# A state space layer on one core: sums moved to identity matmuls and ScalarE copies, ScalarE's work set between exponentials

## The chip, the cores and the metric

The kernel runs on one core of a Trainium2 chip. Its engines work side by side: PE (TensorE, matmuls into PSUM), DVE (VectorE), ACT (ScalarE), POOL (GpSimd), and SP, which here issues the transfers. They pass data through SBUF and PSUM and wait for each other by semaphores. The metric is the device time of one execution in microseconds (us), the median of several.

## The reference

Two layers work one after the other on four images of 384 channels and 64 x 64 positions, in float32. Only the first, a state space layer, is touched by the change. Cut to what matters:

```python
x = x + L0(group_norm(x))
x = x + L1(group_norm(x))            # attention over 7x7 neighbourhoods

def L0(x):                           # L = 4096 positions, D_INNER = 768, D_STATE = 16
    xn = layer_norm(x)
    xb, z = split(xn @ in_proj_w.T)
    xc = silu(causal_conv(xb, 4 taps) + conv_b)
    dt, Bm, Cm = split(xc @ x_proj_w.T)            # 24, 16, 16
    dt = softplus(dt @ dt_w.T + dt_b)
    A = -exp(A_log)
    def step(h, dt_t, B_t, C_t, x_t):              # along the positions
        h = exp(dt_t * A) * h + (dt_t * x_t) * B_t
        return h, sum_n(h * C_t)
    y = scan(step) + xc * D
    return (y * silu(z)) @ out_proj_w.T
```

## The kernel before

The first layer goes through each image in 16 chunks ("steps") of T = 256 positions, 64 steps in all. Channels lie on the partitions, 128 at a time, so the inner width is d = 0..5. For each d the 16 states are taken four at a time (g = 0..3): that makes 24 units m in a step, each of two halves of two states, and 48 "slots". Each slot holds two exponentials and two scans; all other work of the layer, for this chunk and for those before and after it, is put into the slots by a table, and each engine runs it in this order.

The core of a unit:

```python
def driven(I, m, h, eng):       # db = (dt * x) * B, on VectorE or GpSimd
    db = w2.tile([P, NG, T], F32, tag="db", bufs=6)
    dtx = dtx_ps[:, d % 2, :] if eng is nc.vector else h["dtx"][d]
    eng.tensor_tensor(db, dtx.broadcast(...), h["B"][g], ALU.mult)          # L550

def decay(I, m, half, h):       # two exponentials, into one of two PSUM tiles
    da = ps_a.tile([P, 2, T], F32, tag="da")                                # bufs=2
    for k in range(2):
        act(da[:, k, :], h["dt"][d // 2][:, d % 2, :], AF.Exp, scale=nega[:, d, n : n + 1])

def scans(I, m, half, hs):
    for k in range(2):
        nc.vector.tensor_tensor_scan(hs[:, j, :], da[:, k, :], dbs[I, m][:, j, :],
                                     state[:, d, n : n + 1], ALU.mult, ALU.add)  # L571

def with_c(I, m, h, hs):        # on GpSimd
    nc.gpsimd.tensor_copy(state[:, d, g * NG : (g + 1) * NG], hs[:, :, T - 1])   # L580
    nc.gpsimd.tensor_tensor(hs, hs, h["C"][g], ALU.mult)                         # L581

def summed(I, m, h, hs):        # sum over the states: accumulating transposes, L594
    ...

for n in range(STEPS * M):                       # M = 24 units
    I, m = divmod(n, M)
    hs = w2.tile([P, NG, T], F32, tag="hs", bufs=5)
    for half in range(2):
        decay(*nxt, steps[nxt[0]])               # of the half after this one
        if half == 0:
            with_c(*behind[-1])                  # of the unit before this one
            ...                                  # summed() of the unit before that
        scans(I, m, half, hs)
        run(I, 2 * m + half, 2 * m + half + 1)   # what the table has in this slot
```

Softplus, once for each pair of d (q = 0, 1, 2), as max(v, 0) + ln(1 + exp(-|v|)), with what rounding lost in 1 + exp put back:

```python
def project():   # PE: pb = w_dt x dt                                        L491
def parts():     # ACT: e = Abs(pb + bias), r = Relu(pb + bias), for k = 0, 1
def exped():
    act(t["e"], t["e"], AF.Exp, scale=-1.0)
    act(t["pb"], t["e"], AF.Identity, bias=1.0)
def logged():
    act(t["dt"], t["pb"], AF.Ln)
def lost():
    nc.vector.scalar_tensor_tensor(t["pb"], t["pb"], -1.0, t["e"],
                                   ALU.add, ALU.subtract)                 # L514
    nc.vector.tensor_tensor(t["pb"], t["r"], t["pb"], ALU.subtract)       # L517
def added():
    nc.vector.tensor_tensor(t["dt"], t["dt"], t["pb"], ALU.add)           # L520

at(first, project); at(first + 3, parts); at(first + 4, exped)
at(first + 5, logged); at(first + 6, lost); at(first + 7, added)          # first = 34, 36, 46
```

The dt of a pair then goes to GpSimd, too (dtx = dt * xc, L537), and a copy of dtx to PSUM for VectorE (L543). The output projection ends with the residual:

```python
def residual(first, n):
    xo = h["xo"][:, first : first + n, :]
    nc.vector.tensor_tensor(xo, h["po", first][:, :n, :], xo, ALU.add)    # L653
```

Once in a step ScalarE does all its Silu together (`burst`, slot 26): a table load, six instructions of 128x512, and a load of the table with Exp and Ln again. PSUM tiles for everything but da, y and dtx come from one pool of four banks.

Of the kernel before, what the change touches and what calls it, by code (L numbers as in the profile page):

```python
# [14 lines left out]
P = 128  # L15
C = 384
# [32 lines left out]
def two_layers(  # L49
# [74 lines left out]
    make_identity(nc, ident)  # L124
    ones_c = const.tile([P, P], F32, name="ones_c")
# [145 lines left out]
    def layer0(x1s, mvs, gms1):  # L271

        with ExitStack() as es:
# [8 lines left out]
            gms, gbs, st1s = {}, {}, {}  # L282
            dtx_ps = ps_x.tile([P, 2, T], F32, name="dtx_ps")

# [45 lines left out]
            def normed(I, h, at):  # L330
# [10 lines left out]
                def by_group():  # L341
                    h["xn"] = w2.tile([P, NJ, T], F32, tag="xn", name=f"xn_{b}_{i}", bufs=1)
                    for j in range(NJ):
                        act(
                            h["xn"][:, j, :], h["x"][:, j, :], AF.Identity,
                            scale=gms[b][:, j, 1:2], bias=gbs[b][:, j, :],
                        )
# [17 lines left out]

                def root():
                    act(h["var"][:, 0, :], h["var"][:, 0, :], AF.Ln, bias=eps)
                    act(h["var"][:, 0, :], h["var"][:, 0, :], AF.Exp, scale=-0.5)

                at(12, load)  # L370
                at(22, by_group)
                at(24, lambda: mean("xn", "mu"))
                at(26, lambda: with_row("mu", ALU.subtract))
                at(30, square)
                at(31, lambda: mean("sq", "var"))
                at(34, root)
                at(35, lambda: with_row("var", ALU.mult))
# [16 lines left out]
            def with_bias(dst, pb, bias):  # L394

                for k in range(2):
                    act(dst[:, k, :], pb[:, k, :], AF.Identity, bias=bias[:, k : k + 1])

            def prepared(I, h, at):
# [22 lines left out]
                at(-11, kept)  # L422
                for p, (x, c, z) in enumerate((
                    ((-10, -9, -6), (1, 2, 5), (9, 10, 13)),
                    ((-6, -5, -2), (3, 4, 7), (12, 13, 16)),
                    ((-4, -3, 0), (7, 8, 11), (15, 16, 19)),
                )):
                    d = 2 * p
                    pair(("x", p), x, lambda pb, k, d=d: in_proj(pb, k, d + k, h["xn"]))
                    at(x[2], lambda p=p, d=d: with_bias(  # L430
                        xb[:, d : d + 2, KC - 1 :], h["pb"][("x", p)], binp[:, d : d + 2]
                    ))

                    def conv_out(p=p, d=d):
                        c = w2.tile([P, 2, T], F32, tag="xc", name=f"xc_{b}_{i}_{d}", bufs=6)
                        with_bias(c, h["pb"][("c", p)], cvb[:, d : d + 2])
                        h["xc"].append(c)

                    pair(("c", p), c, lambda pb, k, d=d: conv(pb, k, d + k))
                    at(c[2], conv_out)  # L440

                    def z_out(p=p, d=d):
                        z = w2.tile([P, 2, T], F32, tag="sz", name=f"sz_{b}_{i}_{d}", bufs=6)
                        with_bias(z, h["pb"][("z", p)], binp[:, ND + d : ND + d + 2])
                        h["sz"].append(z)

                    pair(("z", p), z, lambda pb, k, d=d: in_proj(pb, k, ND + d + k, h["xn"]))
                    at(z[2], z_out)
# [15 lines left out]
                def rows():  # L464
# [6 lines left out]
                    for tag in "BBBCBCCC":  # L471
# [7 lines left out]
                at(26, burst)  # L479
                at(28, lambda: x_proj((0, 1, 2)))  # L480
                at(29, lambda: x_proj((3, 4, 5)))
                at(32, rows)

                def softplus(q, first):
# [12 lines left out]
                    def parts():  # L497
                        t["e"] = w2.tile([P, 2, T], F32, tag="sp_e", name=f"spe_{b}_{i}_{q}")
                        t["r"] = w2.tile([P, 2, T], F32, tag="sp_r", name=f"spr_{b}_{i}_{q}")
                        for k in range(2):  # L500
                            bias = dtb[:, 2 * q + k : 2 * q + k + 1]
                            act(t["e"][:, k, :], t["pb"][:, k, :], AF.Abs, bias=bias)
                            act(t["r"][:, k, :], t["pb"][:, k, :], AF.Relu, bias=bias)

                    def exped():
                        act(t["e"], t["e"], AF.Exp, scale=-1.0)
                        act(t["pb"], t["e"], AF.Identity, bias=1.0)
# [5 lines left out]
                    def lost():  # L513
                        nc.vector.scalar_tensor_tensor(  # L514
                            t["pb"], t["pb"], -1.0, t["e"], ALU.add, ALU.subtract
                        )
                        nc.vector.tensor_tensor(t["pb"], t["r"], t["pb"], ALU.subtract)  # L517

                    def added():
                        nc.vector.tensor_tensor(t["dt"], t["dt"], t["pb"], ALU.add)  # L520
                        h["dt"].append(t["dt"])

                    at(first, project)
                    at(first + 3, parts)
# [640 lines left out]
```

## Time and profile of the kernel before

| | |
|---|---|
| time, median of 3 | 8366.12 us (8359.93 to 8367.44) |
| span of the profiled execution | 8357.8 us |
| busy: PE, DVE, ACT, POOL | 87%, 87%, 70%, 85% |
| transfers | 583.06 MB, mean 70 GB/s |
| L571, the scans | 5760 with a state to start from, 728 ns mean |
| L581, the product with C | 1536, 2358 ns mean |
| exponentials into da | 6144, 477 ns mean |

Busy time is the time in which at least one instruction of an engine runs. A group's line gives its line in the kernel, the engine and operation, what it writes and reads, the shapes and the count; after the bar the busy time in us and the mean length of one in ns; after the second bar the engine's idle time just before such instructions, and who ended it. The row PEclk is the granted clock of TensorE, as a share of full speed.

### The profile page before, as it was taken

To read this page: it belongs to the slowest core of one execution; us is meant where nothing else is said; L and a number is where in the kernel's file an instruction comes from. 1 tells how busy PE (TensorE), PEld (TensorE's weight loads), DVE (VectorE), ACT (ScalarE), POOL (GpSimd) and SP (SyncE) were. 2 spreads that over 40 slices of the span, in tenths; PEclk is the share of its full clock that TensorE was granted. 3 is DMA by queue.
4 is the path that set the end of the run, shared out by engine and by line. 5 is a ranking of instruction groups with operands and counts; after the bars stand their busy time and mean duration, and the time that the engine had idled before them with its cause. 6 is when DMAs were issued, how large, how long until landed. Compare 5 with 4: busy or idle time off the path is not lost. (4 is left out here: it accounts for less than half of the span.)

```text
span 8357.8 us, 139186 instructions
## 1 busy us (share of the span) xinstructions
PE 7252.0 (87%) x45882; PEld 5495.0 (66%) x45882; DVE 7311.7 (87%) x13300; ACT 5812.2 (70%) x13758; POOL 7092.7 (85%) x5719
## 2 busy tenths in 40 slices
PE   7888888888888888888888888888699999999999
PEld 5776677777666677776777677766555555555555
DVE  5999999999999999999999999999856666666666
ACT  5777777777777777777777777777545455455455
POOL 4999999999999999999999999999767677777677
PEclk9998898889889998899898889989799999999999
DMA  3111211121112111211211111112122232232222
GB/s 112 59 61 66 75 58 55 63 74 58 62 66 74 53 58 66 72 58 64 68 63 53 58 65 60 55 57 71 65 89 86 76 94 88 78 92 85 83 87 65
DMA packets 327504, 583.06 MB, mean 70 GB/s; under 512 B 62940, under 2 KB 211180, under 8 KB 326660
## 3 DMA queue, kind: packets, MB, share of 16 engines
q1 hardware_dynamic: 326788, 574.17, 21.3%
q8 instruction: 370, 6.06, 0.3%
q14 instruction: 346, 2.83, 0.1%
HBM read 471.49 MB, written 84.73 MB: 67 GB/s over the span
## 5 line engine op out<-in xcount | busy, mean ns | idle before, releaser
L571 DVE TENSOR_TENSOR_SCAN hs<-da,state,db 128x256 f32<-128x256 f32 x5760 | 3855.0, 728 | 88.9 <-ACT da L96 64.8
L96 ACT ACTIVATE da<-dt,nega 128x256 f32<-128x256 f32 x6144 | 2917.7, 477 | 1208.2 <-DVE hs L571 1100.8
L581 POOL TENSOR_TENSOR hs<-hs,C 128x1024 f32<-128x1024 f32 x1536 | 3621.7, 2358 | 123.9 <-POOL state L580 0.4
L594 PE MATMUL y<-ident,hs 128*128 128x128 f32 x12288 | 1774.6, 296 | 904.5 <-POOL hs L581 902.3
L594 PEld LDWEIGHTS y<-ident,hs 128*128 128x128 f32 x12288 | 1540.5, 153 | 1207.9 <-POOL hs L581 1098.9
L941 POOL TENSOR_SCALAR sg<-sg,rsum 128x308 f32<-128x308 f32 x1536 | 1619.9, 1073 | 633.8 <-DVE rsum L939 631.8
L550 POOL TENSOR_TENSOR db<-dtx,B 128x1024 f32<-128x1024 f32 x576 | 1360.5, 2362 | 0.1
L550 DVE TENSOR_TENSOR db<-dtx_ps,B 128x1024 f32<-128x1024 f32 x960 | 1141.3, 1199 | 0.0
L382 PE MATMUL mm_ps<-xn,w_in 128*128 128x256 f32 x4608 | 1127.4, 392 | 10.1 <-DVE yg L624 8.1
L96 ACT ACTIVATE sg<-sg,mx 128x308 f32<-128x308 f32 x1536 | 828.7, 541 | 251.3 <-DVE mx L926 236.7
L926 DVE CUSTOM_DVE_ANT_0 sg<-lg_ps,bias 128x308 f32<-128x308 f32 x1536 | 643.1, 475 | 375.1 <-PE lg_ps L920 375.1
L382 PEld LDWEIGHTS mm_ps<-xn,w_in 128*128 128x128 f32 x4608 | 872.5, 197 | 119.1 <-DVE yg L624 8.4
L389 PE MATMUL mm_ps<-xb,dcv 128*128 128x256 f32 x3072 | 783.9, 409 | 0.0
L389 PEld LDWEIGHTS mm_ps<-xb,dcv 128*128 128x128 f32 x3072 | 615.7, 208 | 88.3 <-issue 0.3
L969 ACT COPY tb<-pt_ps 88x512 f32<-88x512 f32 x384 | 222.2, 579 | 624.7 <-PE pt_ps L965 624.7
L580 POOL COPY state<-hs 128x4 f32<-128x4 f32 x1536 | 289.1, 188 | 341.8 <-DVE hs L571 328.0
L639 PE MATMUL mm_ps<-yg,w_out 128*128 128x256 f32 x2304 | 539.8, 385 | 0.0
L956 DVE COPY ta<-pt_ps 110x512 f32<-110x512 f32 x768 | 492.4, 682 | 23.2 <-PE pt_ps L951 23.2
L639 PEld LDWEIGHTS mm_ps<-yg,w_out 128*128 128x128 f32 x2304 | 439.6, 195 | 59.1
L951 PE MATMUL pt_ps<-ident,sg 128*110 128x128 f32 x3072 | 417.7, 279 | 0.8 <-POOL sg L941 0.8
L951 PEld LDWEIGHTS pt_ps<-ident,sg 128*110 128x110 f32 x3072 | 322.7, 133 | 77.9 <-issue 47.6
L824 PE MATMUL mm_ps<-xn,w_qkv 128*128 128x512 f32 (+2 forms) x612 | 270.7, 579 | 60.4 <-DVE xn L811 53.2
(141 smaller groups left out, 9152.5 us busy)
## 6 DMA issues: line engine op xcount, KB each, us to landing
B<-bcrows SPq DMA_DIRECT2D x256, 512.0 KB
C<-bcrows SPq DMA_DIRECT2D x256, 512.0 KB
vw<-vd SPq DMA_DIRECT2D x1792, 33.0 KB
xr<-x SPq DMA_DIRECT2D x28, 1056.0 KB
vd<-v SPq DMA_DIRECT2D x280, 96.0 KB
xi<-in_x_dram SPq DMA_DIRECT2D x64, 384.0 KB
xo<-in_x_dram SPq DMA_DIRECT2D x64, 384.0 KB
x<-xo SPq DMA_DIRECT2D x64, 384.0 KB
```

Of the source, the lines that this page charges most:

```text
L96: ins = nc.scalar.activation(o, i, func, **kw)
L382: nc.tensor.matmul(pb[:, k, :], w_in[:, j, m * P : (m + 1) * P], xn[:, j, :], start=(j == 0), stop=(j == NJ - 1),)
L389: nc.tensor.matmul(pb[:, k, :], dcv[:, d, c, :], xb[:, d, c : c + T], start=(c == 0), stop=(c == KC - 1),)
L550: eng.tensor_tensor(db, dtx.unsqueeze(1).broadcast_to([P, NG, T]), h["B"][g], ALU.mult)
L571: nc.vector.tensor_tensor_scan(hs[:, j, :], da[:, k, :], dbs[I, m][:, j, :], state[:, d, n : n + 1] if I % NCHUNK else 0.0, ALU.mult, ALU.add,
L581: nc.gpsimd.tensor_tensor(hs, hs, h["C"][g], ALU.mult)
L594: nc.tensor.matmul(y[:, d % 2, half, :], hs[:, k, half * P : (half + 1) * P], ident, is_transpose=True, start=(first and half == 0 and d % ...
L639: nc.tensor.matmul(h["po", first][:, m - first, :], w_out[:, d, m * P : (m + 1) * P], h["yg"][d // 2][:, d % 2, :], start=(d == 0), stop=( ...
L926: nc.vector.tensor_tensor_reduce(sg[:, hh, :], lg[:, :NK], bias[:, 4 * m + hh, :], -1.0, BIG, ALU.add, ALU.min, mx[:, hh : hh + 1],)
L941: nc.gpsimd.tensor_scalar(sg[:, hh, :], sg[:, hh, :], rs[:, hh : hh + 1], None, ALU.mult)
L951: nc.tensor.transpose(pt[: KN[c], col : col + P], sg[:, 2 * pair + hh, KOFF[c] : KOFF[c] + KN[c]], ident,)
L956: nc.vector.tensor_copy(t[: KN[0], :, :].rearrange("p a q -> p (a q)"), pt[: KN[0], :])
```

## The change

It takes additions off VectorE. In softplus the parts r, ln and minus the lost part are added up by matmuls with the identity (and with its negative, `nident`) in PSUM, and ScalarE copies the sum to SBUF. The residual, too, is a matmul with the identity, ahead of the output projection in the same accumulation, and ScalarE copies the result. ScalarE takes the copies of the last states from GpSimd. And the table of slots is new: ScalarE's work is cut into single instructions, each with its own slot, and set between the two exponentials of a slot.

```diff
+    nident = const.tile([P, P], F32, name="nident")
+    nc.vector.tensor_scalar(nident, ident, -1.0, None, ALU.mult)
...
+            AT = {
+             'norm': (9, 20, 21, 22, 22, 25, 28, 30, 32, 33, 33),
+             'kept': -11,
+             'x': ((-9, -8, -4, -4), (-6, -6, -3, -2), (-4, -4, -1, 1)),
+             'c': ((1, 1, 5, 6), (3, 4, 8, 8), (8, 9, 13, 13)),
+             'z': ((8, 9, 13, 13), (10, 11, 15, 15), (14, 15, 19, 21)),
+             'burst': (25, 26, 28, 31),
+             'softplus': ((32, 34, 36, 36, 37, 38, 40, 42), (34, 38, 39, 40, 42, 43, 44, 48),
+                          (45, 49, 50, 50, 51, 51, 52, 55)),
+             'dtx': (-5, -1, 8, 17, 19, 33),
+             'dtx_ps': (-3, 4, 13, 20, 24, 36),
+             'driven': ((-5, 0), (-2, 1), (-1, 1), (1, 1), (1, 0), (5, 1), (7, 0), (7, 1),
+                        (11, 0), (14, 1), (14, 0), (16, 1), (19, 0), (21, 1), (23, 0), (25, 1),
+                        (25, 1), (25, 1), (29, 0), (32, 1), (34, 0), (38, 1), (39, 0),
+                        (41, 1)),
+             'turn': (21, 25, 26),
+             'out': (8, 17, 18, 19, 20, 22, 23, 27, 29, 30),
+            }
...
-            driven_at = (
-                (-4, 0), (-1, 1), (1, 1), (2, 1), (4, 0), (7, 1), (8, 0), (10, 1),
-                (12, 0), (15, 1), (17, 1), (18, 1), (20, 0), (22, 1), (24, 0), (26, 1),
-                (26, 1), (26, 1), (30, 0), (33, 1), (36, 0), (39, 1), (40, 0), (43, 1),
-            )
...
-                for p, (x, c, z) in enumerate((
-                    ((-10, -9, -6), (1, 2, 5), (9, 10, 13)),
-                    ((-6, -5, -2), (3, 4, 7), (12, 13, 16)),
-                    ((-4, -3, 0), (7, 8, 11), (15, 16, 19)),
-                )):
...
-                    for tag in "BBBCBCCC":
+                    for tag in "BBBBCCCC":
...
                     def lost():
                         nc.vector.scalar_tensor_tensor(
-                            t["pb"], t["pb"], -1.0, t["e"], ALU.add, ALU.subtract
-                        )
-                        nc.vector.tensor_tensor(t["pb"], t["r"], t["pb"], ALU.subtract)
-
-                    def added():
-                        nc.vector.tensor_tensor(t["dt"], t["dt"], t["pb"], ALU.add)
+                            t["e"], t["pb"], -1.0, t["e"], ALU.add, ALU.subtract
+                        )
+
+                    def summed():
+                        t["sum"] = bank()
+                        for k in range(2):
+                            for n, (one, part) in enumerate(
+                                ((ident, t["r"]), (ident, t["dt"]), (nident, t["e"]))
+                            ):
+                                nc.tensor.matmul(
+                                    t["sum"][:, k, :], one, part[:, k, :],
+                                    start=(n == 0), stop=(n == 2),
+                                )
+
+                    def out():
+                        nc.scalar.copy(t["dt"], t["sum"])
...
+            def kept_states(I, m, hs):
+                d, g = divmod(m, NS // NG)
+                nc.scalar.copy(state[:, d, g * NG : (g + 1) * NG], hs[:, :, T - 1])
+
             def with_c(I, m, h, hs):
-                d, g = divmod(m, NS // NG)
-                nc.gpsimd.tensor_copy(state[:, d, g * NG : (g + 1) * NG], hs[:, :, T - 1])
-                nc.gpsimd.tensor_tensor(hs, hs, h["C"][g], ALU.mult)
+                nc.gpsimd.tensor_tensor(hs, hs, h["C"][m % (NS // NG)], ALU.mult)
...
+                    if ds[0] == 0:
+                        nc.tensor.matmul(po, ident, h["xo"][:, m, :], start=True, stop=False)
...
-                def residual(first, n):
-                    xo = h["xo"][:, first : first + n, :]
-                    nc.vector.tensor_tensor(xo, h["po", first][:, :n, :], xo, ALU.add)
+                def projected(first, n):
+                    nc.scalar.copy(h["xo"][:, first : first + n, :], h["po", first][:, :n, :])
...
                 for half in range(2):
+                    others, acts = plan[I][2 * m + half]
+                    if half == 0 and behind:
+                        acts.insert(0, lambda last=behind[-1]: kept_states(*last[:2], last[3]))
                     if 2 * n + half + 1 < len(halves):
                         nxt = halves[2 * n + half + 1]
-                        decay(*nxt, steps[nxt[0]])
+                        acts.insert(0, lambda nxt=nxt: decay(*nxt, 0, steps[nxt[0]]))
+                        acts.insert(2, lambda nxt=nxt: decay(*nxt, 1, steps[nxt[0]]))
+                    for what in acts:
+                        what()
...
                     scans(I, m, half, hs)
-                    run(I, 2 * m + half, 2 * m + half + 1)
+                    for what in others:
+                        what()
```

In the old slots of x, c and z (`for p, (x, c, z)`) the first two are the matmuls and the third ScalarE's instructions; in the new tables the first two numbers are the slots of the matmuls and the last two those of ScalarE's instructions; the eight of softplus are: projection, Abs and Relu, Exp, 1 + e, Ln, the lost part, the sum, the copy.

## The prediction

> **What bounds the kernel now.** I read the busy shares of the page first, then its 40 slices.
>
> ```profile
> PE 7252.0 (87%) x45882; PEld 5495.0 (66%) x45882; DVE 7311.7 (87%) x13300; ACT 5812.2 (70%) x13758; POOL 7092.7 (85%) x5719
> ...
> DVE  5999999999999999999999999999856666666666
> ACT  5777777777777777777777777777545455455455
> POOL 4999999999999999999999999999767677777677
> PEclk9998898889889998899898889989799999999999
> ```
>
> The shares say nothing: they average two layers. The slices split them. Up to slice 29, the state space layer, VectorE is at nine tenths or more; then comes the attention layer, bounded by TensorE, which the change doesn't touch. So the question is what one chunk ("step") of the first layer costs, and there are 4 x 16 = 64 of them.
>
> Second view: groups of instructions between 2000 and 4000 us (inside the first layer), and the busy time of two stretches. In the stretch rows the columns are length, then PE, PEld, DVE, ACT and POOL busy, clock, DMA share, GB/s.
>
> ```profile
> 2000.00:3000.00 1000.00, 842.42 (x4422) 698.08 (x4421) 983.69 (x1431) 788.05 (x1722) 918.65 (x691) 0.89 0.19 65
> 3000.00:4000.00 1000.00, 844.54 (x4419) 699.60 (x4418) 982.09 (x1433) 786.39 (x1719) 921.44 (x692) 0.89 0.19 64
> ```
>
> ```profile
> L571 DVE TENSOR_TENSOR_SCAN hs<-da,state,db 128x256 f32<-128x256 f32 x1976 | 1322.5, 728 | 28.0 <-ACT da L96 20.2 <-POOL hs L581 5.2
> L581 POOL TENSOR_TENSOR hs<-hs,C 128x1024 f32<-128x1024 f32 x518 | 1221.6, 2358 | 41.7
> L96 ACT ACTIVATE da<-dt,nega 128x256 f32<-128x256 f32 x2074 | 985.4, 477 | 404.7 <-DVE hs L571 368.8 <-DVE gmean_b L262 0.7 <-DVE gmean_a L262 0.6
> L594 PE MATMUL y<-ident,hs 128*128 128x128 f32 x4144 | 594.1, 294 | 300.9 <-POOL hs L581 300.4
> ...
> L580 POOL COPY state<-hs 128x4 f32<-128x4 f32 x518 | 97.6, 188 | 118.2 <-DVE hs L571 112.3 <-PE mm_ps L389 4.2 <-DVE gmean_a L262 0.9
> ...
> L517 DVE TENSOR_TENSOR mm_ps<-spr,mm_ps 128x512 f32<-128x512 f32 x65 | 45.2, 696 | 2.2
> ...
> L520 DVE TENSOR_TENSOR dt<-dt,mm_ps 128x512 f32<-128x512 f32 x65 | 43.3, 666 | 0.0
> ```
>
> A step has 24 products with C (L581), so 518 of them are 21.58 steps in 2000 us: **92.7 us a step**. Dividing the busy sums by 21.58 gives per step DVE 91.1, POOL 85.3, PE 78.2, ACT 73.0. VectorE is the bound; it idles 1.6 us, of which 1.1 on exponentials (23.5 us of waits on da in this stretch). ACT waits for scans (17 us a step) and PE waits for POOL (14): they have room, but how much, and where, is the question.
>
> Third view: VectorE's timeline, start and length. It gives queue time, start to start, which is what a removed instruction really gives back.
>
> ```profile
> 3059.08 0.69 DVE L514 SCALAR_TENSOR_TENSOR mm_ps<-mm_ps,spe 128x512 f32<-128x512 f32 x1
> 3059.80 0.70 DVE L517 TENSOR_TENSOR mm_ps<-spr,mm_ps 128x512 f32<-128x512 f32 x1
> 3060.40 1.39 DVE L571 TENSOR_TENSOR_SCAN hs<-da,state,db 128x256 f32<-128x256 f32 x2
> 3061.71 0.66 DVE L520 TENSOR_TENSOR dt<-dt,mm_ps 128x512 f32<-128x512 f32 x1
> 3062.28 1.38 DVE L571 TENSOR_TENSOR_SCAN hs<-da,state,db 128x256 f32<-128x256 f32 x2
> ```
>
> L517 lasts 0.70 but holds the queue 0.60, as tails overlap; L520 0.57.
>
> **What the Trainium skill says.** "TensorE: Matmul & The Clock Gate", Part 1: the array runs at half or full clock by its recent activity. The trace agrees: in stretches of 4 us the granted clock is mostly 1.00, and falls to 0.54 to 0.61 after PE waits of some 3 us. So more matmuls partly pay for themselves by fewer cold stretches. "ScalarE: Activation LUTs", What ACT_TABLE_LOAD costs: an ACTIVATE without pointer operands is 186 ns + 0.833 ns per element, back-to-back ones overlapping by some 93 ns. The trace has 202 ns for a 32x1 ACTIVATE and 577 ns for a 128x512 copy, near that. "PSUM — Partial Sum Buffer", Specifications: GpSimd has no access to PSUM. Here POOL reads dt (L537), so a sum made on TensorE has to be copied to SBUF; that copy is the price of the change. No run yet shows it.
>
> **Part by part, in us a step.**
>
> VectorE. Three L517 at 0.63 (with the gap of 0.03 ahead) are 1.9; three L520 at 0.57 are 1.7; the two residual additions (L653) hold 0.58 and 0.31, 0.9. The tables of db places have 15 on VectorE before and 14 after, one db at 1.11 start to start. Sum 5.6: 91.1 - 5.6 = **85.5**.
>
> POOL. 24 state copies of 0.188 go (4.5), with some 0.08 of gap each (1.9); one db of 2.36 comes. 85.3 - 4.5 + 2.4 = **83.2**. Its product with C now waits for ScalarE's state copy, instead of following its own.
>
> ScalarE. 24 state copies: 0.20 from the 32x1 ACTIVATE, less an overlap of about 0.07, 3.1. Three copies of sums at 0.48 start to start (that of ys, L605), 1.4; residual copies 0.48 + 0.30, 0.8. Sum 5.3: 73.0 + 5.3 = **78.3**.
>
> TensorE. 18 identity matmuls for the sums and 3 for the residual, 256 columns each. A matmul of this kind appears as two records (1548 for 36 x 21.58 of L382), and twelve start within 2.60 us at full clock, so 0.216 each: 42 x 0.216 = 9.1. 78.2 + 9.1 = **87.3** if the clock stays as it is. At full clock the work is less: 192 transposes at 0.11 and 204 wide records at 0.216, with small ones some 67, after it 76.
>
> So no engine stands over 88, VectorE stays the longest that can't shrink, and all four lie within 10 us. The gain is 5.6 less what the tighter coupling costs:
>
> Exponentials. Two PSUM tiles hold da, so ScalarE can be only about one half unit (two scans) ahead. I laid the queue times on the 48 slots of a step. An example: before, slot 38 has two exponentials (0.92 start to start in the timeline), Exp and Identity of softplus (0.64 and 0.54), 2.1 on ACT, against two scans, 1.28, on DVE. Slots 37 to 39 together, with eight Abs and Relu at 0.355, an Ln at 0.48 and one db, are the worst block: ACT 7.3, DVE 5.0; there the trace indeed has a wait of 0.86. After, softplus is spread: slots 36 to 38 have ACT 6.9, DVE 5.6. But the burst of Silu has 6.8 against 5.5 (before 6.8 against 6.1), and slots 2 and 13 have 2.2 and 2.7 against 1.3. I choose 2.0 of idle for 1.1.
>
> TensorE's lateness. The sums come in PE's order behind transposes that wait for POOL, and ScalarE's copy stands between two exponentials. Slots 40 to 47 hold 17.7 of PE work at full clock in about 14.7 of time, and slot 4, with the third sum, 5.2 more; the copy is due three slots (5.5 us) later. I take 0.7.
>
> With 0.5 for what else VectorE waited for: 85.5 + 2.0 + 0.7 + 0.5 = 88.7, a saving of 4.0; times 64 it is 256 us. As the slots look chosen with care, I round up to 266: 8366 - 266 = **8100**.
>
> **The rivals.** *ScalarE becomes the bound by order, not by sum*: 78.3 of 88.7 with hardly any lead. For it: the waits on da that exist already; against: smaller pieces and a place between exponentials. If its waits reach 4.5, the step is 91.2 and the time 8270, within 2%. *TensorE becomes the bound*: 87.3 at the old clock, with gaps that can't all be filled. For it: the local overload; against: a busier array should be granted more clock, and the copies were given more distance (conv and z three to five slots from their last matmul, before three). If it adds 3 the step is 91 as well, 8255. *POOL starves at the burst*: the state copy queues behind 5.8 us of Silu and table loads, so its product starts up to 5 us late; its 83.2 would then become 88. It costs little as long as POOL arrives at the burst with a backlog. *The schedule is better than I grant*: idle as before, 1.6, gives 87.1, 5.6 x 64 = 358, 8008.
>
> **Range and chances.** 2% is 167 us, or 2.6 a step: a step under 90.1. My middle is 88.6. A rival would have to take back over half of the 5.6 to miss it; a loss of 2% would need a step over 95.3, that is 10 us of new waits. Range 7990 (6 a step saved) to 8220 (2.3 saved). Faster by over 2%: 0.75; within: 0.20; slower: 0.05.
>
> **What would show it.** Right: VectorE 85 to 86 busy a step, L517's, L520's and L653's work gone; POOL near 83; ACT near 78, with waits on hs down from 17 to near 9; clock in the layer up from 0.89 to 0.91 or more; a step of 88 to 89; the attention layer unchanged. Wrong: VectorE waiting over 4 a step for da, with ACT in turn waiting for PE's mm_ps (TensorE late) or not waiting at all (ScalarE full); or a state copy far longer than 0.2; or POOL waiting for ACT's state over 5 a step.

## The result, and the profile after

The changed kernel takes 8264.29 us (8263.57 to 8272.73) against 8366.78 before: a ratio of 0.9881, 95% interval 0.9864 to 0.9898. It is faster by 1.2%, 102 us; 266 were predicted, and the range ended at 8220.

First the slices of the page after, in the same order as before.

```profile
PE 7509.9 (91%) x48570; PEld 5817.5 (70%) x48570; DVE 6989.3 (85%) x12725; ACT 5890.7 (71%) x15613; POOL 6982.6 (85%) x4247
...
DVE  5999999999999999999999999999666666666666
ACT  5888888888888887888878888888455455455455
POOL 4999999999999999999999999999677777677777
PEclk9999999999999999999999999999899999999999
```

VectorE still stands at nine tenths or more through the first layer, TensorE's clock is up, and the attention layer is as it was. The tenths hide the difference. Two stretches of 1000 us inside the layer show it (columns as before: length; PE, PEld, DVE, ACT, POOL busy; clock).

```profile
2000.00:3000.00 1000.00, 901.91 (x4974) 767.89 (x4974) 947.40 (x1357) 814.11 (x2071) 918.25 (x452) 0.94 0.20 64
3000.00:4000.00 1000.00, 901.50 (x4977) 768.50 (x4978) 945.64 (x1364) 816.18 (x2076) 920.96 (x453) 0.94 0.20 66
```

A step ends in one load of the Exp and Ln table; 58 steps lie between the same two of these loads in both traces. That gives 90.9 us a step after ((5797.7 - 526.4) / 58) and 92.5 before ((5897.0 - 532.7) / 58), a more exact figure than the 92.7 of the prediction. Of the 90.9, VectorE is busy 94.65%, 86.0 us, and **idle 4.9**; before it was busy 90.9 and idle 1.6. So the change took 4.9 us of work off VectorE and gave it 3.3 us of new waiting. 64 x 1.6 is the 102 us.

The waits between 2000 and 4000 us say where it stands now (engine, what waited, for whom; us in total, times, longest).

```profile
ACT da L96 <- DVE hs L623: 284.3, 397, 3.3
...
POOL hs L635 <- ACT state L631: 154.8, 183, 3.9
PE y L648 <- POOL hs L635: 111.0, 98, 2.2
...
PE y L648 <- ACT ys L659: 86.0, 23, 6.2
ACT xb L96 <- PE mm_ps L409: 52.9, 22, 3.4
DVE yg L678 <- PE mm_ps L671: 52.3, 48, 2.6
DVE hs L623 <- issue: 35.3, 46, 1.2
...
DVE hs L623 <- ACT da L96: 8.3, 25, 1.3
```

There are 22 steps in it. VectorE waits 2.4 a step for TensorE ahead of the gating (L678), a wait that didn't exist, and 2.0 ahead of scans: 0.4 named as a wait for da, and 1.6 that the profile calls "issue" and which end, in the timeline, when an exponential does. Another 0.4 is for Ln and for the layer norm's means. ScalarE, in its turn, waits 2.4 a step for TensorE's input projection, and TensorE 3.9 for ScalarE's copy of y.

The waits for exponentials have two sources. Followed back along ScalarE's timeline, 10.3 us of them (22 waits, 0.5 a step) come behind ScalarE's wait for the input projection, as here:

```profile
3022.32 0.47 ACT L96 ACTIVATE xb<-mm_ps,binp 128x256 f32<-128x256 f32 x1 [2.41 <-PE mm_ps L409]
3022.70 0.87 ACT L96 ACTIVATE da<-dt,nega 128x256 f32<-128x256 f32 x2
3023.26 2.43 DVE L623 TENSOR_TENSOR_SCAN hs<-da,db 128x256 f32<-128x256 f32 x4 [0.42 <-issue]
```

The other 1.5 a step follow no wait for TensorE, and that is about what the kernel before had (1.1 by the waits named, 1.5 followed back in the same way).

Two timelines show the wait at the gating as it happens. VectorE:

```profile
3010.09 1.38 DVE L623 TENSOR_TENSOR_SCAN hs<-da,state,db 128x256 f32<-128x256 f32 x2
3012.80 0.69 DVE L678 TENSOR_TENSOR yg<-mm_ps,sz 128x512 f32<-128x512 f32 x1 [1.33 <-PE mm_ps L671]
3013.41 1.38 DVE L623 TENSOR_TENSOR_SCAN hs<-da,state,db 128x256 f32<-128x256 f32 x2
```

TensorE in the same stretch, one line for each run of records:

```profile
3001.77 3.63 PE L648 MATMUL y<-ident,hs 128*128 128x128 f32 x16 [3.41 <-ACT ys L659]
...
3007.41 0.60 PE L558 MATMUL mm_ps<-spr,ident 128*128 128x256 f32 x2
3007.84 0.59 PE L558 MATMUL mm_ps<-dt,ident 128*128 128x256 f32 x2
...
3009.57 0.59 PE L558 MATMUL mm_ps<-spe,nident 128*128 128x256 f32 x2
3010.00 1.46 PE L409 MATMUL mm_ps<-xn,w_in 128*128 128x256 f32 x6
3011.30 0.38 PE L666 MATMUL mm_ps<-ident,ys 128*128 128x128 f32 x2
3011.51 0.60 PE L671 MATMUL mm_ps<-xc,dsd 128*128 128x256 f32 x2
3011.95 0.38 PE L666 MATMUL mm_ps<-ident,ys 128*128 128x128 f32 x2
3012.17 0.60 PE L671 MATMUL mm_ps<-xc,dsd 128*128 128x256 f32 x2
```

The scans end at 3011.47. The gating needs the matmuls of L671, which end at 3012.77. Close ahead of these stand, in TensorE's order, six new identity matmuls, 2.6 us from start to start, and three of the input projection, 1.3. What came off VectorE stands ahead of VectorE's next input, on another engine. A second delay is in the same queue: TensorE had waited 3.41 for ScalarE's copy of y, its clock was 0.65 from 3001 to 3007 (1.00 from 3007 to 3013), and from 3001.77 on it had no gap. That is the rule here: 48.0 of the 52.3 us of waits at the gating come while TensorE runs, since a wait for the copy of y, without a gap (of 0.15 or more), for 27 us on average, of which 5.2 are identity matmuls. e6 below takes these matmuls out.

### The profile page after: what moved, and what is told of

Same layout as the page of the kernel before. It is cut to its first block, busy times and chain, and to the rows that moved or that the text cites. A ratio compares the mean times of both kernels' runs of the same rounds, so it can differ in the third digit from the quotient of the medians.

```text
span 8262.0 us, 144369 instructions
## 1 busy us (share of the span) xinstructions
PE 7509.9 (91%) x48570; PEld 5817.5 (70%) x48570; DVE 6989.3 (85%) x12725; ACT 5890.7 (71%) x15613; POOL 6982.6 (85%) x4247
## 5 line engine op out<-in xcount | busy, mean ns | idle before, releaser
L623 DVE TENSOR_TENSOR_SCAN hs<-da,state,db 128x256 f32<-128x256 f32 x5760 | 3850.5, 730 | 121.2 <-issue 90.9
L648 PE MATMUL y<-ident,hs 128*128 128x128 f32 x12288 | 1730.3, 293 | 589.4 <-POOL hs L635 354.7
L648 PEld LDWEIGHTS y<-ident,hs 128*128 128x128 f32 x12288 | 1516.8, 151 | 885.3 <-POOL hs L635 517.4
L600 POOL TENSOR_TENSOR db<-dtx,B 128x1024 f32<-128x1024 f32 x640 | 1514.2, 2366 | 5.1
L600 DVE TENSOR_TENSOR db<-dtx_ps,B 128x1024 f32<-128x1024 f32 x896 | 1065.5, 1201 | 0.7 <-ACT dtx_ps L593 0.7
L416 PE MATMUL mm_ps<-xb,dcv 128*128 128x256 f32 x3072 | 716.2, 379 | 0.0
L416 PEld LDWEIGHTS mm_ps<-xb,dcv 128*128 128x128 f32 x3072 | 572.7, 190 | 75.5 <-issue 0.3
L978 PE MATMUL lg_ps<-k,q 32*128 32x308 f32 x3072 | 311.4, 473 | 0.0
```

What stands on the lines that cost most here:

```text
L416: nc.tensor.matmul(pb[:, k, :], dcv[:, d, c, :], xb[:, d, c : c + T], start=(c == 0), stop=(c == KC - 1),)
L600: eng.tensor_tensor(db, dtx.unsqueeze(1).broadcast_to([P, NG, T]), h["B"][g], ALU.mult)
L648: nc.tensor.matmul(y[:, d % 2, half, :], hs[:, k, half * P : (half + 1) * P], ident, is_transpose=True, start=(first and half == 0 and d % ...
```

## The experiments

Each is an edit of the changed kernel unless said. "Step" is from the table loads; busy and idle are VectorE's, from the stretches 2000 to 4000 us, applied to the step, each rounded by itself. Ratios are to the kernel before.

| run | us | ratio (95%) | step | busy | idle |
|---|---|---|---|---|---|
| before | 8366.78 | 1 | 92.5 | 90.9 | 1.6 |
| changed | 8264.29 | 0.9881 (0.9864 to 0.9898) | 90.9 | 86.0 | 4.9 |
| e1 gating later | 8227.18 | 0.9835 (0.9819 to 0.9852) | 90.3 | 85.7 | 4.6 |
| e2 ys at 19 | 8366.88 | 1.0002 (0.9993 to 1.0011) | 92.5 | 85.8 | 6.7 |
| e5 states on GpSimd | 8363.73 | 0.9997 (0.9989 to 1.0006) | 92.3 | 86.2 | 6.1 |
| e6 softplus sum on VectorE | 8371.65 | 1.0008 (0.9999 to 1.0016) | 92.5 | 89.6 | 2.9 |
| e9 one of three matmuls | 8163.41 | 0.9759 (0.9742 to 0.9777) | 89.3 | 86.1 | 3.2 |
| e10 no state copies | 8245.55 | 0.9857 (0.9841 to 0.9872) | 90.6 | 85.9 | 4.6 |
| e11 gating and x later | 8173.53 | 0.9770 (0.9755 to 0.9786) | 89.5 | 85.7 | 3.7 |
| e12 gating later, ys at 20 | 8217.62 | 0.9823 (0.9807 to 0.9839) | 90.2 | 85.6 | 4.6 |
| e13 residual on VectorE | 8286.55 | 0.9904 (0.9890 to 0.9919) | 91.2 | 87.0 | 4.2 |
| e14 exponentials together | 8435.48 | 1.0082 (1.0067 to 1.0097) | 93.5 | 86.4 | 7.2 |
| e15 gating, x later, ys at 20 | 8167.91 | 0.9763 (0.9747 to 0.9779) | 89.3 | 85.6 | 3.7 |
| e16 new slots, old operations | 8507.76 | 1.0170 (1.0155 to 1.0185) | 94.9 | 90.3 | 4.7 |
| e17 e11 and one of three | 8091.21 | 0.9670 (0.9656 to 0.9685) | 88.2 | 85.6 | 2.6 |
| e18 before, gating one slot after | 8397.88 | 1.0038 (1.0025 to 1.0051) | 92.9 | 91.3 | 1.6 |
| e19 old slots, old operations, interposed | 8446.18 | 1.0096 (1.0079 to 1.0113) | 93.8 | 91.3 | 2.5 |
| e20 old slots, new operations | 8390.26 | 1.0029 (1.0019 to 1.0040) | 92.9 | 87.1 | 5.7 |

My theory was that TensorE, which has more to do and runs in its order, hands over late; the first rival that ScalarE's order is the limit; the second that GpSimd, waiting for ScalarE's state copies, holds up everything behind it.

### Where VectorE waits: the gating one slot after its matmuls (e1)

```diff
-             'turn': (21, 25, 26),
+             'turn': (21, 25, 29),
```

> The changed kernel with one number changed: the gating multiplication by silu(z) on VectorE comes at slot 29 of its pair instead of 26, so four slots after TensorE's turning back (slot 25) and not one. In the changed kernel VectorE waits there for TensorE 52.3 us in 2000, 2.4 us a step of 90.9. Theory (TensorE is late in its own order and VectorE stands right behind it): this wait goes, the step falls by 1.5 to 2.4, the time by 100 to 150 us to about 8115 to 8165. Rival (ScalarE's exponentials are the real limit, the wait only stands where another would stand): VectorE's idle moves to the waits on da, the time stays within 30 us of 8264.

It took 8227, 37 us less: more than the rival allows, far less than the theory. The waits of this kernel tell why:

```profile
ACT xb L96 <- PE mm_ps L409: 102.8, 38, 4.9
...
DVE hs L623 <- issue: 73.4, 52, 2.9
```

The wait at the gating is gone, but ScalarE's wait for the input projection has grown from 52.9 to 102.8, and VectorE's ahead of scans from 35.3 to 73.4. Followed back as above, 50.4 us of VectorE's waits for exponentials now come behind ScalarE's wait for x, in place of 10.3. TensorE is still late, and the next one to need it waits: ScalarE's copy of x, with an exponential behind it, and VectorE behind that. A wait that was removed at one consumer was taken over by the next.

### The next consumer, too (e11), and TensorE's load (e9, e17)

```diff
-             'x': (..., (-4, -4, -1, 1)),
+             'x': (..., (-4, -4, 1, 3)),
-             'turn': (21, 25, 26),
+             'turn': (21, 25, 29),
```

> The changed kernel with gating at slot 29 of its pair as in the first experiment (8227), and ScalarE's two copies of the third pair of x, which come three and five slots after their matmuls, two slots later each (1 and 3 in place of -1 and 1). With the gating moved alone ScalarE waits there for TensorE 102.8 us in 2000, 4.6 a step, and VectorE in turn for exponentials 4.1. Theory (the wait only moved from VectorE to ScalarE's queue): this wait falls below 2 a step, VectorE's idle by about 2, the time by 80 to 130 us, to 8100 to 8150. Rival: TensorE's load itself is the limit, more distance brings less than 40 us.

8173.53: 54 us below e1 and 91 below the changed kernel, between what the two expected. That three numbers of the table are worth almost as much again as the whole change (102 us) is the plainest result here.

```profile
DVE hs L623 <- issue: 33.4, 32, 1.2
ACT sz L96 <- PE mm_ps L409: 31.5, 24, 1.4
...
ACT xb L96 <- PE mm_ps L409: 5.7, 9, 1.4
```

In these three lines of its waits the one for x has shrunk from 102.8 to 5.7, and that ahead of scans from 73.4 to 33.4; the one for z has come up, from 6.6 to 31.5, and 3.7 a step of idle are left.

e9 takes the load off instead of the distance up. It leaves out two of the three matmuls of each softplus sum, so its dt isn't softplus; every other engine runs what it ran.

```diff
-                                ((ident, t["r"]), (ident, t["dt"]), (nident, t["e"]))
+                                ((ident, t["dt"]),)
```

> The changed kernel, with only one of the three identity matmuls of each softplus sum (that of the logarithm); the part max(v, 0) and the lost part are computed as before but left out of the sum, so dt is not softplus. ScalarE, VectorE and GpSimd run the same instructions; TensorE loses 24 records of 0.216, 5.2 us a step. Theory (TensorE's load, not the engines around it, makes the waits): VectorE's idle of 4.9 a step falls to 2.5 or less, the time by 130 us or more, to 8135 or below. Rival 1 (ScalarE's order is the limit): within 40 us of 8264. Rival 2 (GpSimd, late for its wait on the state copies, holds everything): within 40 us of 8264 too, with TensorE waiting longer for it.

8163.41, 101 us less. I had expected at least 130, the rivals at most 40. Its waits:

```profile
PE y L648 <- POOL hs L635: 151.1, 114, 2.2
...
DVE yg L678 <- PE mm_ps L671: 28.3, 49, 1.3
...
ACT xb L96 <- PE mm_ps L409: 15.5, 21, 1.6
```

TensorE's waits on GpSimd rose, from 111.0 to 151.1, as it is ready sooner; the two waits for TensorE fell, from 52.3 to 28.3 and from 52.9 to 15.5, and VectorE's idle by 1.7. So what went of the waits, 1.7 of 3.3, was made by the load of TensorE, and not by GpSimd's pace, nor by ScalarE's, whose instructions are the same.

e17 has the edits of e11 and of e9.

> Gating and x later (8173) together with only one of the three identity matmuls of each softplus sum; the part max(v, 0) and the lost part are left out of the sum, so dt is not softplus. TensorE loses 5.2 us a step. Theory (the idle that is left, 3.7 a step, is mostly TensorE's load): idle falls to 2 or less, the time by 90 us or more, to 8080 or below. Rival (what is left is the order of ScalarE's work and GpSimd): within 40 us of 8173.

Both together take 8091.21, 82 us below e11 where I had said at least 90; the idle is 2.6 and not 2. Of the 3.3 us of new waiting, 2.2 are thus traced to TensorE's lateness: 1.1 by more distance, another 1.1 by less load. In e17 the two largest waits on VectorE's list that the kernel before didn't have are 15.1 us in the stretch (0.7 a step) for TensorE's means in the layer norm and 5.9 (0.3) for Ln; they make up the 1.0 that is left.

### The rivals alone (e10, e5)

```diff
+    nc.gpsimd.memset(state, 0.0)
...
-                        acts.insert(0, lambda last=behind[-1]: kept_states(*last[:2], last[3]))
```

This leaves out the copies of the states, so the recurrence starts anew in each chunk.

> The changed kernel without the copies of the last states: each chunk starts from a state of zero, so the recurrence is cut at chunk borders. ScalarE loses 2.4 us a step of queue time, GpSimd no longer waits for it (7.0 a step). Theory (TensorE): a small gain, at most 60 us, 8205 or above. Rival 1 (ScalarE) and rival 2 (GpSimd held by ScalarE): the step falls by 2 to 4, the time by 130 us or more, to 8135 or below; GpSimd's wait tells which: if ScalarE still waits for scans over 10 a step, it was not ScalarE.

8245.55, 19 us less. GpSimd's 7.0 us a step of waiting for these copies, long as they look in the table of waits, cost next to nothing, and ScalarE's 24 copies little: 0.3 a step together. So the state copies are out as the main cause, by way of GpSimd and of ScalarE. ScalarE's order as such isn't tested by this; e14 does that.

```diff
             def with_c(I, m, h, hs):
+                d, g = divmod(m, NS // NG)
+                nc.gpsimd.tensor_copy(state[:, d, g * NG : (g + 1) * NG], hs[:, :, T - 1])
                 nc.gpsimd.tensor_tensor(hs, hs, h["C"][m % (NS // NG)], ALU.mult)
...
-                        acts.insert(0, lambda last=behind[-1]: kept_states(*last[:2], last[3]))
```

> The changed kernel with the copies of the last states back on GpSimd, all else kept. ScalarE loses 24 copies that hold its queue 0.10 each, 2.4 us a step; GpSimd gets back 24 x 0.27 = 6.5, but no longer waits for ScalarE (154.8 us in 2000, 7.0 a step, in the changed kernel). Rival 1 (ScalarE is the limit): the step falls by some 2, to about 8130. Rival 2 (GpSimd is held up by ScalarE's state copies and passes it on to TensorE): same or faster. Theory (TensorE): GpSimd has 90 of 90.9 to do, TensorE gets its input later still: same to slower by up to 100 us, 8260 to 8360.

8363.73, 99 us slower and just above what the theory allowed; GpSimd is busy 94.8% of a step. A copy holds ScalarE's queue 0.10 us and GpSimd's 0.27; in this schedule moving the copies is worth about as much as the whole change.

### The other parts undone (e6, e13)

```diff
                     def lost():
                         nc.vector.scalar_tensor_tensor(
-                            t["e"], t["pb"], -1.0, t["e"], ALU.add, ALU.subtract)
+                            t["pb"], t["pb"], -1.0, t["e"], ALU.add, ALU.subtract)
+                        nc.vector.tensor_tensor(t["pb"], t["r"], t["pb"], ALU.subtract)
                     def summed():
-                        (six identity matmuls)
+                        nc.vector.tensor_tensor(t["dt"], t["dt"], t["pb"], ALU.add)
-                        nc.scalar.copy(t["dt"], t["sum"])
```

> The changed kernel with the two additions of softplus back on VectorE, in the slots of the lost part and of the sum; the 18 identity matmuls and three ScalarE copies of a step go, all else is kept. TensorE loses 36 records of 0.216, 7.8 us a step, VectorE gets 3.6, ScalarE loses 1.5. By queue time alone VectorE goes from 86.0 to 89.6 busy. Theory (TensorE is late): VectorE's idle of 4.9 falls to some 2, so the step is about 91.5 and the time within 60 us of the changed kernel, 8240 to 8320: the identity matmuls brought almost nothing. Rival (ScalarE): idle falls only by what ScalarE loses, step 92.5 to 93.5, 8370 to 8430.

8371.65. The time is where the rival had put it, at its lower edge, and not where the theory had: busy came back to 89.6 as worked out, but idle fell only to 2.9, not to 2. That is 2.0 less, between the 1.5 of the rival and the 2.9 of the theory. The identity matmuls do bring 107 us in this schedule, just under half of what their 3.6 us a step on VectorE promise (230 us). The rest is the 2.0 us a step of idle that they cause. Two of its waits:

```profile
PE y L640 <- ACT ys L651: 128.4, 43, 5.6
...
DVE yg L670 <- PE mm_ps L663: 19.4, 14, 2.0
```

TensorE waits longer for the copy of y than in the changed kernel (86.0), and VectorE still waits less at the gating (52.3 there). TensorE now catches up first: only 0.4 of the 19.4 us come while it runs without a gap since a wait for the copy. So that wait makes TensorE late at the gating only together with the identity matmuls.

```diff
-                    if ds[0] == 0:
-                        nc.tensor.matmul(po, ident, h["xo"][:, m, :], start=True, stop=False)
...
-                    nc.scalar.copy(h["xo"][:, first : first + n, :], h["po", first][:, :n, :])
+                    xo = h["xo"][:, first : first + n, :]
+                    nc.vector.tensor_tensor(xo, h["po", first][:, :n, :], xo, ALU.add)
```

> The changed kernel with the residual addition back on VectorE, in the slots of its ScalarE copies. TensorE loses 6 records of 0.216, 1.3 us a step, ScalarE 0.8, VectorE gets 0.9. Theory (TensorE's load makes the waits): VectorE's idle falls by about what TensorE loses, so nothing changes: 8264 within 30 us. Rival (every part off VectorE pays by its queue time): 0.9 x 64 = 58 us slower, 8322. The two are 60 us apart, so this is the weakest of the tests.

It is 8286.55, 22 us slower, within what the theory allowed: 1.0 us more busy, 0.7 less idle. Again part of it is given back.

### ScalarE's order (e2, e12, e15, e14)

TensorE's wait for the copy of y looked like a cause of its lateness, so I moved that copy ahead.

```diff
-             'turn': (21, 25, 26),
+             'turn': (19, 25, 26),      # e2
+             'turn': (20, 25, 29),      # e12; e15 has the third pair of x at 1 and 3 besides
```

> The changed kernel with one number changed: ScalarE's copy of y to SBUF comes at slot 19 of its pair instead of 21. The one PSUM bank of y is then free earlier; in the changed kernel TensorE waits for this copy 86 us in 2000, 3.9 us a step, most of it at the second pair. Theory (TensorE's lateness is what counts): TensorE's wait falls below 1 a step, and as it is late afterwards, VectorE's wait for the gating input and ScalarE's for TensorE shrink by a half; the time falls by 40 to 120 us. But the copy may itself come too early for the last transposes and make ScalarE wait: then no gain. Rival (ScalarE): no change beyond 30 us.

> The changed kernel with gating at slot 29, and ScalarE's copy of y at slot 20, which is where it was before the change, in place of 21 (19 alone made the kernel slower by 102 us). With gating alone at 29 TensorE waits for this copy 3.0 us a step. Theory: at 20 the transposes of the pair are through and ScalarE has not yet the Exp and Ln of softplus ahead of it, so TensorE starts earlier where it is most loaded: 8227 falls by 20 to 80 us. Rival: the copy made ScalarE wait at 19 since TensorE itself is late there; then 20 is slower too, 8250 or above.

> Gating at 29, the third pair of x two slots later (together 8173), and the copy of y at 20 in place of 21. At 20 TensorE waited for the copy 0.4 us a step less, and the time fell by 10 us where x was not moved. Theory (TensorE's start after the wait matters only where TensorE is late): 8173 falls by 0 to 40 us, to 8133 to 8173. If it rises, ScalarE's bunch of softplus around slot 36 has become the tighter spot.

e2 is a miss: 103 us slower. TensorE's wait for ScalarE is gone from its list, but ScalarE now waits 25.3 for TensorE's last transposes, TensorE's wait for GpSimd rises from 111.0 to 171.9, and VectorE's ahead of scans from 35.3 to 69.0. Which of these sets off the others wasn't settled. But with no wait for the copy of y at all, VectorE still waits 40.0 us at the gating, now behind TensorE's waits for GpSimd. At slot 20 the gain is 10 us in e12, below what I expected, and 6 in e15, within it. There TensorE's wait for the copy fell from 67.2 to 58.1 and from 76.7 to 40.1: where the distances were mended, half of this wait was worth 6 us. What it is worth in the changed kernel itself, with its load, wasn't shown. e15, at 8167.91, is the fastest of the kernels that leave nothing out: a ratio of 0.9763 (0.9747 to 0.9779) to before, where the changed kernel has 0.9881.

```diff
-                        acts.insert(2, lambda nxt=nxt: decay(*nxt, 1, steps[nxt[0]]))
+                        acts.insert(1, lambda nxt=nxt: decay(*nxt, 1, steps[nxt[0]]))   # e14
```

> The changed kernel with the two exponentials of a half next to each other, as before the change, and ScalarE's other work behind them. In the trace two exponentials in a row hold the queue 0.46 to 0.50 each, one with another instruction behind it 0.40; so the interposing saves ScalarE up to 0.08 x 96 = 7.7 us a step, which would be why its busy time came out at 74.1 and not 78.3. If so: ScalarE 2 to 5 us busier a step, VectorE waiting for exponentials 1 to 3 longer, 8264 becomes 8330 to 8450. If ScalarE's order has room (the theory of TensorE alone): within 30 us of 8264.

8435.48, 171 us slower, within what was expected if ScalarE's order has no room, but not by the waits that I had named: those ahead of scans fell from 43.6 us to 26.8 in the stretch. Here ScalarE's timeline before the change and after it are worth a look side by side. Before, two exponentials and the start of what follows, 0.93 later:

```profile
3002.36 0.99 ACT L96 ACTIVATE da<-dt,nega 128x256 f32<-128x256 f32 x2 [0.29 <-DVE hs L571]
3003.29 0.82 ACT L96 ACTIVATE xc<-mm_ps,cvb 128x256 f32<-128x256 f32 x2
```

After, with the state copy set between them, 0.92:

```profile
3002.41 0.47 ACT L96 ACTIVATE da<-dt,nega 128x256 f32<-128x256 f32 x1
3002.81 0.19 ACT L631 COPY state<-hs 128x4 f32<-128x4 f32 x1
3002.92 0.48 ACT L96 ACTIVATE da<-dt,nega 128x256 f32<-128x256 f32 x1
3003.33 0.46 ACT L96 ACTIVATE spe<-mm_ps,dtb 128x256 f32<-128x256 f32 x1
```

The two exponentials write the same tile, and the second waits for the end of the first by a semaphore: it starts 0.51 later in both (before, a pair takes 0.99 and one of them 0.48). With an instruction that doesn't wait for it, an exponential holds the queue 0.40. (My 0.46 to 0.50 were halves of a pair.) A copy of 0.11 fits into the gap, and in this place it costs ScalarE nothing. Over a step the 24 copies aren't free: without them ScalarE is busy 2.2 less in e10 and 2.0 in e5. In e14 ScalarE is busy 2.7 us more a step, and VectorE waits 3.8 for the gating instead of 2.4 and 1.0 for Ln instead of 0.3.

### Slots and operations apart (e16, e18, e19, e20)

e16 has the changed kernel's table and interposing, with all three kinds of operations as before (the edits of e5, e6 and e13 together).

> The new table of slots and the spread of ScalarE's work alone: softplus additions and residual on VectorE, last states copied by GpSimd, as before the change. VectorE has 91.1 less one db, 90.0 busy a step; GpSimd 85.3 + 2.4 and its small gaps, near 90. Theory (the waits come from TensorE's added load): with TensorE back at some 78, VectorE idles 1.5 to 2.5 and the time lies within 50 us of before, 8320 to 8410. Rival (the new slots themselves are bad, gating one slot behind its matmuls above all): VectorE's idle stays near 4.9, step 94.9, 8520.

8507.76, as the rival had it: with TensorE at 85% and its clock at 0.85, VectorE still waits 2.0 a step for the gating and 1.0 for the layer norm's mean.

```profile
DVE yg L672 <- PE mm_ps L665: 41.5, 36, 1.7
```

The new table isn't good by itself. But distance alone isn't the whole of it, as the kernel before shows with just one number changed:

```diff
-                at(s + 4, gated)
+                at(s + 2, gated)
```

> The kernel before with one number changed: gating one slot after the turning back, as in the changed kernel, in place of three. TensorE has 78 of 92.5 us to do there. Theory (the distance has to cover TensorE's place in its order, full or not): VectorE waits for the gating input 1 to 2.4 us a step and the time rises by 50 to 150 us, to 8415 to 8515. Rival (only a loaded TensorE is late): within 30 us of 8366.

8397.88, 31 us slower, below what the theory said and at the edge of the rival; VectorE waits 0.7 a step there.

```profile
DVE yg L624 <- PE mm_ps L617: 16.0, 13, 1.8
DVE hs L571 <- ACT da L96: 5.1, 16, 0.6
```

Its idle in all is the same 1.6, since its wait for da fell from 23.5 to 5.1. So in the old table one slot costs little. e16 has the same matmuls to do and waits 2.0 there, so TensorE's own load isn't all that counts: followed back, all 41.5 us of e16 come behind TensorE's waits for GpSimd, which has the state copies again and is busy 87.3 a step, in place of 83.6. Which part of the new table makes that worse than e18's 0.7 wasn't tested.

e19 and e20 have the table of before, e19 with the old operations and e20 with the new ones, both with ScalarE's work interposed. (The tiles of B and C are fetched in the new order in both, as in all edits of the changed kernel; this wasn't tested alone.) The main places, cut:

```diff
-             'softplus': ((32, 34, 36, 36, 37, 38, 40, 42), (34, 38, 39, 40, 42, 43, 44, 48), ...),
+             'softplus': ((34, 37, 38, 38, 39, 40, 41, 43), (36, 39, 40, 40, 41, 42, 43, 45), ...),
-             'turn': (21, 25, 26),
+             'turn': (20, 21, 24),
...
+             x, c, z, norm, burst, dtx, driven and out with the slots of before
```

> The operations of before in the slots of before, but ScalarE's work cut up and set between the exponentials by the changed kernel's loop. ScalarE's queue time falls (two exponentials in a row hold 0.46 to 0.50 each, with another instruction between 0.40), but VectorE waited only 1.1 us a step for exponentials. Theory (VectorE's own work is the limit before): 0 to 70 us faster, 8295 to 8366. Rival (interposing is what the change lives on): 100 us or more faster, below 8266.

> The operations of the changed kernel and its interposing, in the slots of before: gating three slots after its matmuls, the third pair of x three slots, the sums two slots ahead of their copies, 15 db on VectorE. VectorE has 86.0 + 1.1 = 87.1 a step. Theory (distance): its idle is 2.5 to 4, the step 89.6 to 91.1, the time 8180 to 8275, no slower than the changed kernel: the new slots brought nothing. Rival (the new slots are fitted to the new operations): idle above 5, the time above 8310.

My theory missed both; for e20 the rival's figures came. e19 is 79 us slower than before, although ScalarE is busy 2.2 us less a step: VectorE's waits for da double (23.5 to 49.0 in the stretch), and what stands between two exponentials does delay the tile that both fill, though that this is the cause is only argued. e20 has the 87.1 busy that I had worked out, but 5.7 of idle, of which 4.3 is the wait for da.

```profile
DVE hs L622 <- ACT da L96: 92.8, 109, 2.0
ACT dt L563 <- PE mm_ps L557: 51.5, 44, 2.8
```

Here ScalarE waits for the sums' matmuls, which stand two slots ahead of their copies (14.7 us in the changed kernel), and 36.7 us of VectorE's waits for exponentials come behind that: TensorE's lateness once more, at a third consumer.

With ScalarE's work interposed in all four, the times in us are:

| | old operations | new operations |
|---|---|---|
| old slots | 8446 (e19) | 8390 (e20) |
| new slots | 8508 (e16) | 8264 (changed) |

The new operations bring 56 us in the old slots and 243 in the new; the new slots cost 62 with the old operations and bring 126 with the new. Interposing costs 79 with slots and operations of before (e19) and brings 171 in the changed kernel (e14). The three kinds of operations nearly add up: undoing the states costs 99, the softplus sum 107, the residual 22, and all three at once 243. Table and interposing can't be priced alone.

## Why the prediction was wrong, point by point

- **VectorE**: 5.6 us less work expected, 85.5 busy; measured 86.0, against 90.9. Right to half a us. The saving is 4.9 and not 5.6; some 0.4 of the difference is that the scans hold the queue a little longer, 62.6 a step from start to start.
- **GpSimd**: 83.2 expected, 83.6 measured (91.96% of 90.9). Right. Its wait for the state copies was 7.0 a step, above the 5 that I had put down as a sign of failure; e10 shows that the sign was badly chosen, for the wait costs 0.3 at most.
- **ScalarE**: 78.3 expected, 74.1 measured. The new instructions were right within 0.6: from start to start they hold the queue 4.7 a step, of 5.3 expected. What I left out is that the exponentials then hold it 41.2 in place of 43.9, as other work fills the gap ahead of the second of a tile; e16 and e19, interposed with the old operations, have 70.4 and 70.6 busy against 72.8 before. I had the exponentials in a row in the timeline and didn't ask what would fill the gap.
- **TensorE**: 87.3 at an unchanged clock, and the clock to rise to 0.91 or more; it is 82.0 at 0.94. The direction was right. The clock follows recent activity, says "TensorE: Matmul & The Clock Gate" of the Trainium skill in Part 1, and here it was 0.89 with TensorE busy 84% before, and 0.94 with 90% after. The number of matmuls alone doesn't set it: e16 has those of before and 0.85.
- **Exponentials**, 2.0 of idle: 2.0 (0.4 and 1.6 of the two kinds of waits). The number is luck in part: I had put the rise from 1.1 down to ScalarE's fuller slots, but 0.5 of it comes behind TensorE, and in e9, where ScalarE has the same to do, these waits are 1.4.
- **TensorE's lateness**, 0.7: **this is the step that failed.** I had looked for it at the copies of the sums and taken 0.7. It is 2.4 on VectorE's own list, at the gating, and 0.5 of the 2.0 ahead of scans comes from it through ScalarE: 2.9. Taking TensorE's load off (e9) or giving its consumers more distance (e11) brings back 1.7 and 1.1 of idle, both 2.2. I looked at the slots of sums, conv and z, found their distances long enough, and didn't look at 'turn': gating went from three slots after its matmuls to one. The table was in front of me: (21, 25, 26). The copies of the third pair of x kept their three slots and were late all the same.
- The sum: 85.5 + 2.0 + 0.7 + 0.5 was 88.7, and it is 90.9: 0.5 by busy time, 1.7 by waits, which is the 2.4 at the gating in place of 0.7. Rounding the gain up on trust in chosen slots went the wrong way. Three slips in the working change nothing in this: conv and z have four to six slots from their last matmul and not three to five; 8100 is a step of 88.5, not 88.6; and a step of 95.3 takes 9.8 us of waits in all, 8.2 of them new.
- **The rivals**: "TensorE becomes the bound", with 3 added and 8255, is what came: 8264. (8270, of "ScalarE becomes the bound by order", is as near, but it rests on 4.5 of waits for exponentials, and they are 2.0.) I had held a higher clock and more distance against it, and the first of these is true but doesn't help an engine that works in order and is late at one point of the step.

What isn't settled: the chain behind e2, where one copy two slots earlier costs 103 us, and behind e19; and what TensorE's wait for the copy of y, with the low clock after it, is worth in the changed kernel by itself. A table fitted to e15's distances as a whole wasn't tried.

## What to carry to other kernels

When work moves from the engine that bounds a kernel to one with room, ask what stands behind it in the second engine's order, and how many us lie between that and its consumer; the sum of busy time doesn't show it, and a wait that is mended at one consumer turns up at the next. Price such a change by the wait as well as by the work: here 4.9 us a step were saved, and 3.3 came back. And where an instruction waits for the end of the one before it, as the second exponential of a tile does here, the gap has room for a small one: doing without this interposing cost ScalarE 2.7 us a step in e14.

## What the runs showed of the hardware

- A ScalarE copy of 128x4 lasts 184 ns but holds the queue 0.10 to 0.11 us when others stand around it; on GpSimd the same copy holds it 0.27 us.
- Two exponentials of 128x256 into one PSUM tile, of which the second waits for the first, start 0.51 us apart, in a row and with a state copy between; followed by an instruction that doesn't wait for it, one holds the queue 0.40.
- A float32 identity matmul of 128x256 appears as two records, 0.43 us from start to start at full clock; six of them, for a sum of three tiles of 128x512, take 2.6 us, about twice the 1.2 of the two VectorE additions that they replace.
